# A two-layer graph network on one core: the second eviction of a transpose, a small copy, and the marks that pace a transform

## The chip, the cores and the metric

The kernel runs on one core of a Trainium2 chip. A core has four engines that matter here: TensorE (PE in the profile: matrix products and transposes), VectorE (DVE), ScalarE (ACT) and GpSimd (POOL). SyncE (SP) only issues transfers. Each engine runs its own queue of instructions in order, and waits where an operand or a buffer isn't ready. The metric is the device time of one execution in microseconds (us).

## What is computed

There are 64 graphs of 256 nodes with 256 channels, all in f32. Layer 0 multiplies by a normalised adjacency matrix and by a weight, adds the input, and applies layernorm. Layer 1 has a convolution over the nodes, a distance-weighted message sum, and a GRU cell. Cut to its core, layer 1 reads:

```python
xc = jnp.transpose(x, (0, 2, 1))
h = relu(_bn(_conv1d(xc, conv1_w, 0), ...))
h = _bn(_conv1d(h, conv2_w, 8), ...)              # 17 taps along the nodes
x_conv = jnp.transpose(relu(h + xc), (0, 2, 1))
s = x @ w_se.T + b_se                             # 3 columns
sq = jnp.sum(s * s, axis=-1)
dist = sq[:, :, None] + sq[:, None, :] - 2.0 * jnp.einsum('bnd,bmd->bnm', s, s)
A = jnp.exp(-dist) * mask
msg = relu(x @ w_msg.T + b_msg)
x_nmp = jnp.einsum('bnm,bmd->bnd', A, msg)
x_in = jnp.concatenate([x_conv, x_nmp], axis=-1)
# GRU cell with input x_in and state x, residual, layernorm
```

## The kernel before

**Tiles and stages.** A tile has 128 partitions, so a graph of 256 nodes is two chunks, and the 256 channels are two halves. The 64 graphs are worked in four quarters of 16. The 17-tap convolution of a quarter is done as a transform in 48 points: each graph's `dft` (L485) fills its columns of `V`, twelve steps of products (L544) multiply by the transformed taps, and a transform back on VectorE (`complex_end`, with outputs stored by SP at L731) gives `xc_d`. The GRU (`gru`, L842 to L921) then takes the quarter graph by graph.

**Software pipeline.** The stages of neighbouring quarters overlap. `graphs` (L970) interleaves the pieces of layer 1 of graph g with the pieces of layer 0 of graph g+2. The graphs of quarter 0 run up to about 305 us. Then quarter 0's product steps run with three pieces of the next graphs in each, to about 420 us. Then come the rest of those graphs (up to graph 27) with the transform back paced between them, to about 533 us. In the later quarters the GRU of a quarter (`late`), six graphs of the next (`begin`) and the transform back run together. The last quarter has no graphs left: only GRU and transform back. While V is in use, the next graphs' dft goes into a second tile `V2` (twelve graphs in quarter 0, six later), and `copies` (L1069) moves it to V by ScalarE copies at L1075 at the end of the transform back.

**One graph of layer 1.** `x1_transposed` (L428) transposes layer 0's result on PE (L434) into one PSUM bank and evicts it in two halves into `xn`. ScalarE evicts half 0 at L435, with a scale and a bias per partition that set one channel to a constant (the row that carries the biases). ScalarE evicts half 1 at L436 with a plain copy. `layer1` then runs conv (L451: 256 columns for h and 3 for s, in one bank for each chunk of nodes), evicts h with a ReLU (ScalarE L454) and copies the three s columns into four column groups of `scols` (VectorE L455). It squares and sums s (VectorE L459, L461, L462), computes msg (L470, evicted at L473), dft (L485, evicted at L490), transposes scols (`p_rows`, L498, evicted at L500 by ScalarE and L502 by VectorE), computes the distances (L509, L510, L511), and the message sum (`p_nmp`, L518, evicted at L522).

**Layer 0 around it.** Adjacency sums (ScalarE L362), transposes (`p_adjT` L384, evicted at L385), the scaled input (L397), products `p_hT` (L405, L410) and `p_out` (L415, L420). A `layernorm` follows, which passes from VectorE (L326 to L328) to GpSimd (power -0.5, L329), back to VectorE (L337) and to ScalarE (L339, two instructions). That x, two graphs ahead, isn't the one that conv reads at that time, but both layernorm and evictions are in the same queues.

**Banks.** The pool `ps` has four PSUM banks in rotation. Within a graph dft's first bank is the one that conv's first chunk had, so dft waits until both readers of conv, L454 and L455, are done.

**Order.** A scheduler places the instructions; the order of the code is a wish for it. Hard order comes from data and buffers, and from `tc.issue_after(op)`, which puts the instructions traced inside it behind `op` where they are on the same engine as `op`. `mark(op, gates)` notes an operation. `paced` (L952) adds, for each mark, a rate to an account (`RATES`, L1065: one rate for marks of graphs, one for marks of the GRU), and for each whole piece due it traces one piece of the transform back, or one copy L1075, behind the marked operation. Marked per graph are the two additions L420, the two ReLUs L454, msg's ReLU L473 and the product L511; in a GRU step the copy L869 (on ScalarE), and VectorE's L876, L898 and L916. Small weight preparations of the GRU (L1021, L1030) also go behind the latest mark.

Of the kernel before, what the change touches and what calls it, by code (L numbers as in the profile page):

```python
# [10 lines left out]
AF = mybir.ActivationFunctionType  # L11
ALU = mybir.AluOpType
AX = mybir.AxisListType

P = 128
# [11 lines left out]
def kernel(  # L27
# [27 lines left out]
    nc = tc.nc  # L55
    B, N, D = x.shape
    TAPS = conv2T.shape[1]
    PAD = TAPS // 2
    NSE = w_seT.shape[1]
# [22 lines left out]
    def bank(name):  # L82
        return ps.tile([P, 512], F32, tag="bank", name=name)

    def accbank(name):
        return psacc.tile([P, 512], F32, tag="acc", name=name)
# [4 lines left out]
    def mark(op, gates=0):  # L91
        marks.append((op.ins, gates))
# [47 lines left out]
    unit, others_only = ident[:, 0:1], const.tile([P, 1], F32, name="others_only")  # L140
# [287 lines left out]
    def x1_transposed(g):  # L428
        x1 = X1.pop(g)
        xn = XN[g] = work.tile([P, 2 * DCH, N], F32, name="xn")  # L430
        p = bank("p_x1T").rearrange("p (k n) -> p k n", k=DCH)
        for k in range(DCH):
            for c in range(NCH):
                nc.tensor.transpose(p[:, k, c * P : (c + 1) * P], x1[:, c, k * P : (k + 1) * P], ident)  # L434
        nc.scalar.activation(xn[:, 0], p[:, 0], AF.Identity, bias=unit, scale=others_only)  # L435
        nc.scalar.copy(xn[:, 1], p[:, 1])  # L436

    def layer1(g, place):

        if g not in XN:  # L440
            x1_transposed(g)
        xn, adjT = XN.pop(g), ADJT.pop(g)
        x1T = xn[:, :DCH]
        yield

        h = work.tile([P, NCH, D], F32, name="h", bufs=1)
        cols = scols.rearrange("p c (q r) -> p c q r", r=32)
        for c in range(NCH):
            p = bank("p_conv1")[:, : D + NSE]
            for k in range(DCH):  # L450
                nc.tensor.matmul(  # L451
                    p, x1T[:, k, c * P : (c + 1) * P], wc1[:, k, :], start=k == 0, stop=k == DCH - 1
                )
            mark(nc.scalar.activation(h[:, c, :], p[:, :D], AF.Relu))  # L454
            nc.vector.tensor_copy(cols[:, c, :, :NSE], p[:, D:].unsqueeze(1).to_broadcast([P, 4, NSE]))  # L455

        s3 = cols[:, :, 0, :NSE]
        sq3 = small.tile([P, NCH, NSE], F32, name="sq3")
        nc.vector.scalar_tensor_tensor(sq3, s3, -1.0, s3, op0=ALU.mult, op1=ALU.mult)  # L459
        nsq = small.tile([P, NCH], F32, name="nsq")  # L460
        nc.vector.tensor_reduce(nsq, sq3, AX.X, ALU.add)  # L461
        nc.vector.tensor_scalar(  # L462
            cols[:, :, 2:4, NSE], nsq.unsqueeze(2).to_broadcast([P, NCH, 2]), 0.5, None, op0=ALU.mult
        )
        yield
        msg = work.tile([P, NCH, D], F32, name="msg", bufs=1)
        p = bank("p_msg").rearrange("p (c d) -> p c d", c=NCH)
        for c in range(NCH):
            for k in range(DCH):
                nc.tensor.matmul(  # L470
                    p[:, c, :], x1T[:, k, c * P : (c + 1) * P], wmsg[:, k, :], start=k == 0, stop=k == DCH - 1
                )
        mark(nc.scalar.activation(msg, p, AF.Relu))  # L473
        yield


        mid = GT // 2
        if TILES[0] is not V:
            AWAY.append(place)
        for k in range(DCH):  # L480
            p = bank("p_dft")

            for c, t0, t1 in ((0, 0, mid + 1), (1, mid - 1, GT)):
                first = t0 + 1 - c * mid
                nc.tensor.matmul(  # L485
                    p[:, t0 * FL : t1 * FL], h[:, c, k * P : (k + 1) * P],
                    fwd[:, first : first + t1 - t0, :].rearrange("p t f -> p (t f)"),
                    start=c == 0, stop=True, skip_group_check=c == 1,
                )
            nc.scalar.copy(  # L490
                TILES[0][:, :, k, place * GT : (place + 1) * GT],
                p[:, : GT * FL].rearrange("p (t f) -> p f t", f=FL),
            )

        yield
        p = bank("p_rows")
        for c in range(NCH):
            nc.tensor.transpose(p[:, c * P : (c + 1) * P], scols[:, c, :], ident)  # L498
        dl = work.tile([64, N], F32, name="dist_l", bufs=1)
        nc.scalar.copy(dl, p[0:64, :N])  # L500
        dr = work.tile([64, N], F32, name="dist_r", bufs=1)
        nc.vector.tensor_copy(dr, p[64:P, :N])  # L502
        yield

        aT = work.tile([P, NCH, 2, P], F32, name="aT", bufs=1)
        for c in range(NCH):
            rows = slice(32 * c, 32 * c + 32)
            p = bank("p_dist")[:, :N]
            nc.tensor.matmul(p, dl[rows, c * P : (c + 1) * P], dr[rows, :], start=True, stop=True)  # L509
            nc.scalar.activation(aT[:, c].rearrange("p n q -> p (n q)"), p, AF.Exp, bias=nsq[:, c : c + 1], scale=2.0)  # L510
        mark(nc.vector.tensor_mul(aT, aT, adjT[:, :, 0:3:2, :]))  # L511
        yield
        if g in ALONE:
            x1_transposed(g + 1)
        p = bank("p_nmp").rearrange("p (k n) -> p k n", k=DCH)
        for k in range(DCH):
            for mc in range(NCH):
                nc.tensor.matmul(  # L518
                    p[:, k, :], msg[:, mc, k * P : (k + 1) * P], aT[:, mc].rearrange("p n q -> p (n q)"),
                    start=mc == 0, stop=mc == NCH - 1,  # L520
                )
        nc.scalar.copy(xn[:, DCH:], p)  # L522
        nc.scalar.dma_start(xn_d[g], xn)
        yield
# [21 lines left out]
    def half(p):  # L546
        return p.rearrange("p (j o) -> p j o", j=2)
# [294 lines left out]
    def gru(g):  # L842
# [5 lines left out]
        trz = gate.tile([P, 4, D], F32, name="trz", bufs=1)  # L848
# [11 lines left out]
        p15, p26 = accbank("p_rz"), accbank("p_rz")  # L860
# [5 lines left out]
        if following:  # L866
            sent(g + 1)
        first = gate.tile([P, 2, D], F32, name="first", tag="gn")
        mark(nc.scalar.copy(first, half(p15)), 1)  # L869
        nc.vector.tensor_add(trz[:, 0:2], first[:, 0:1].to_broadcast([P, 2, D]), half(p26))  # L870
        p7, p34 = accbank("p_rz"), accbank("p_rz")
        block(p7, 0, S[:, 2], T3)
        block(p34, 0, S[:, 3], B22)
# [10 lines left out]
        for c in range(NCH):  # L884
# [5 lines left out]
            p = accbank("p_n")  # L890
# [79 lines left out]
    def graphs(first, part, others):  # L970


        for i in part:
            load(first + i + 3)
            given = {"layer0": layer0(first + i + 2) if first + i + 2 < B else iter(()), "other": others[i]}
            for piece, _ in enumerate(layer1(first + i, i)):
                yield
                for name in PLACES[piece]:
                    if next(given[name], "end") != "end":
                        yield  # L980
            yield from given["other"]
# [64 lines left out]
    def gates(q, part):  # L1046

        for i in part:
            if i == 0:
                load_conv(q * Q)  # L1050
                load_gate(q * Q)
                yield
                load_conv(q * Q + 1)
                sent(q * Q)
                yield
                transposed(q * Q)
                yield
                input_sums(q * Q)
                yield
            yield from gru(q * Q + i)  # L1060
# [18 lines left out]
    for q in range(NQ):  # L1079
        first = (q + 1) * Q  # L1080
# [100 lines left out]
```

## Time and profile before

| what | value |
|---|---|
| median of 3 runs | 2153.79 us (2152.71 to 2159.55) |
| the profiled execution | 2154.62 us |
| its span in the trace | 2152.8 us |
| mean granted TensorE clock | 0.989 |

Busy time by stage, from the trace's windows (us):

| stage | from, to | PE | DVE | ACT | POOL |
|---|---|---|---|---|---|
| graphs of quarter 0 | 0, 305 | 266.49 | 139.02 | 169.81 | 120.40 |
| products of quarter 0 | 305, 420 | 113.73 | 85.53 | 44.37 | 12.21 |
| transform back, paced | 420, 533 | 99.70 | 80.47 | 67.80 | 25.69 |
| next graphs, first GRU | 533, 600 | 56.82 | 28.36 | 35.10 | 27.52 |
| quarter 1 | 600, 1060 | 447.27 | 313.14 | 183.99 | 137.39 |
| its end | 1060, 1170 | 106.89 | 53.20 | 57.09 | 33.88 |
| quarter 2 | 1170, 1660 | 476.33 | 322.97 | 204.73 | 145.99 |
| quarter 3 | 1660, 2153 | 476.27 | 369.67 | 137.15 | 194.19 |

The difference between a stage's length and its PE time is what PE stood idle. In the lines of the profile below, "L451" is line 451 of the kernel before, `out<-in` are tiles by their names, `x8` is the number of instructions, and a bracket at the end of a line gives the engine's idle time before it and the operation that ended it. In a table of groups the numbers are the busy time in us, the mean of one in ns, and the idle time before the group with its releasers.

### The profile page before, as it was taken

The numbers are of one execution on the slowest core, as the hardware profiler recorded it, in microseconds if no ns is written. First come the engines' busy times: TensorE is split into PE (matmuls) and PEld (weight loads), VectorE is DVE, ScalarE is ACT, GpSimd is POOL, SyncE is SP. The second block draws the span as 40 slices with busy tenths as digits, with TensorE's granted clock in tenths as the row PEclk, the third lists the DMA queues.
The fourth block names the chain that finished last, engine by engine and source line by source line (L and its number), as shares of the span: only waits on it lengthen the run. The fifth ranks groups of instructions, "written<-read, shape, count | busy, mean of one in ns | idle before, by whom it ended". The sixth has DMA issues, their size and how long they took to land. (4 is left out here: it accounts for less than half of the span.)

```text
span 2152.8 us, 29120 instructions
## 1 busy us (share of the span) xinstructions
PE 2043.5 (95%) x9693; PEld 1739.9 (81%) x9693; DVE 1392.4 (65%) x3531; ACT 900.0 (42%) x2049; POOL 697.3 (32%) x672
## 2 busy tenths in 40 slices
PE   6999999988899999999999999999999999999998
PEld 5777778876788888777888888877878888888887
DVE  5444458766457887764445878775544889976665
ACT  4566553456442223455554123445554122233332
POOL 3444411122332234223322223323232114355553
PEclk9999999999899999999999999999999999999999
DMA  4666556534437644334334664334332755443331
GB/s 126 212 196 194 164 162 222 173 128 137 108 103 215 204 127 128 125 102 109 104 103 147 207 190 117 113 118 122 104 98 71 240 164 143 112 123 98 88 95 49
DMA packets 302916, 298.23 MB, mean 139 GB/s; under 512 B 84112, under 2 KB 281572, under 8 KB 302766
## 3 DMA queue, kind: packets, MB, share of 16 engines
q1 hardware_dynamic: 242814, 200.37, 31.0%
q10 hardware_dynamic: 44480, 67.39, 9.0%
q0 software_dynamic: 15472, 28.61, 6.0%
q8 instruction: 77, 1.26, 0.2%
q14 instruction: 73, 0.60, 0.1%
HBM read 193.19 MB, written 103.06 MB: 138 GB/s over the span
## 5 line engine op out<-in xcount | busy, mean ns | idle before, releaser
L856 PE MATMUL p_rz<-wrz,sums 128*128 128x256 f32 x1536 | 350.7, 381 | 4.1 <-DVE gn L899 4.1
L893 PE MATMUL p_n<-wn,inputs 128*128 128x256 f32 x1536 | 351.7, 382 | 0.1
L856 PEld LDWEIGHTS p_rz<-wrz,sums 128*128 128x128 f32 x1536 | 291.2, 191 | 47.1 <-issue 8.2
L893 PEld LDWEIGHTS p_n<-wn,inputs 128*128 128x128 f32 x1536 | 289.0, 191 | 43.6 <-issue 6.3
L856 PE MATMUL p_rz<-wrz,inputs 128*128 128x256 f32 x1152 | 271.4, 380 | 1.9 <-ACT inputs L818 1.9
L856 PEld LDWEIGHTS p_rz<-wrz,inputs 128*128 128x128 f32 x1152 | 217.9, 190 | 31.6 <-ACT inputs L818 2.1
L329 POOL TENSOR_TENSOR ln_rs<-ln_rs,neg_half 128x2 f32<-128x2 f32 x129 | 98.6, 764 | 417.4 <-DVE ln_rs L328 363.0
L544 PE MATMUL p_k<-u,VM 128*128 128x256 f32 x736 | 174.5, 380 | 1.5 <-DVE VM L587 0.9
L905 ACT ACTIVATE nn<-gn 128x256 f32<-128x256 f32 x128 | 53.3, 417 | 278.6 <-DVE gn L902 278.4
L451 PE MATMUL p_conv<-wc,xn 128*128 128x259 f32 x512 | 134.9, 397 | 34.5 <-ACT xn L436 29.1
L375 POOL TENSOR_TENSOR dis<-deg,neg_half 128x2 f32<-128x2 f32 x64 | 47.7, 746 | 351.7 <-DVE deg L373 338.3
L835 POOL TENSOR_TENSOR sums<-inputs 128x384 f32<-128x384 f32 x64 | 65.1, 1018 | 285.8 <-ACT inputs L826 224.5
L544 PEld LDWEIGHTS p_k<-u,VM 128*128 128x128 f32 x736 | 138.8, 190 | 21.7 <-DMA u<-ud 1.6
L398 POOL TENSOR_TENSOR x_t<-x_t,b_t 128x512 f32<-128x512 f32 x64 | 86.2, 1347 | 183.1 <-ACT x L397 127.5
L451 PEld LDWEIGHTS p_conv<-wc,xn 128*128 128x128 f32 x512 | 95.1, 193 | 60.6 <-ACT xn L436 39.6
L485 PE MATMUL p_dft<-fwd,h 128*128 128x240 f32 x512 | 117.5, 373 | 18.5 <-DVE scols L455 18.5
L339 ACT ACTIVATE x_g<-x_g,ln_mr,ln_rs 128x256 f32<-128x256 f32 x128 | 70.0, 593 | 146.5 <-DVE ln_mr L337 146.5
L405 PE MATMUL p_hT<-adjT,x 128*128 128x256 f32 x512 | 125.3, 389 | 3.8 <-DVE adjT L387 1.5
L470 PE MATMUL p_msg<-wmsg,xn 128*128 128x256 f32 x512 | 124.7, 388 | 0.2 <-ACT inputs L826 0.2
L415 PE MATMUL p_out<-w,hT 128*128 128x256 f32 x512 | 123.3, 384 | 1.6 <-ACT hT L410 0.7
L511 DVE TENSOR_TENSOR aT<-aT,adjT 128x512 f32<-128x512 f32 x64 | 44.3, 692 | 121.1 <-ACT aT L510 121.1
L485 PEld LDWEIGHTS p_dft<-fwd,h 128*128 128x128 f32 x512 | 97.3, 192 | 30.9 <-DVE scols L455 22.8
(164 smaller groups left out, 3840.9 us busy)
## 6 DMA issues: line engine op xcount, KB each, us to landing
u<-ud SPq DMA_DIRECT2D x284, 256.0 KB
xn_d<-xn ACTq DMA_DIRECT2D x64, 512.0 KB
inputs<-xn_d SPq DMA_DIRECT2D x64, 512.0 KB
ud<-u_set POOLq DMA_DIRECT2D x39, 480.0 KB, 5.8
adj_t<-in_adj_dram SPq DMA_DIRECT2D x64, 256.0 KB
x_t<-in_x_dram SPq DMA_DIRECT2D x64, 256.0 KB
x_d<-x ACTq DMA_DIRECT2D x64, 256.0 KB
xc_d<-VM SPq DMA_DIRECT2D x64, 256.0 KB
```

Of the source, the lines that this page charges most:

```text
L329: nc.gpsimd.tensor_tensor(rs[:, : len(chunks)], rs[:, : len(chunks)], neg_half[:, : len(chunks)], op=ALU.pow)
L339: nc.scalar.activation(y[:, c, :], y[:, c, :], AF.Identity, bias=mr[:, c : c + 1], scale=rs[:, c : c + 1])
L398: nc.gpsimd.tensor_tensor(x_t, x_t, b0_t.unsqueeze(1).to_broadcast([P, NCH, D]), op=ALU.add)
L405: nc.tensor.matmul(p[:, k, :], x1[:, mc, k * P : (k + 1) * P], adjT[:, mc, 1 - mc : 3 - mc, :].rearrange("p n q -> p (n q)"), start=mc == ...
L415: nc.tensor.matmul(p[:, c, :], hT[:, k, c * P : (c + 1) * P], w0[:, k, :], start=k == 0, stop=k == DCH - 1)
L451: nc.tensor.matmul(p, x1T[:, k, c * P : (c + 1) * P], wc1[:, k, :], start=k == 0, stop=k == DCH - 1)
L470: nc.tensor.matmul(p[:, c, :], x1T[:, k, c * P : (c + 1) * P], wmsg[:, k, :], start=k == 0, stop=k == DCH - 1)
L485: nc.tensor.matmul(p[:, t0 * FL : t1 * FL], h[:, c, k * P : (k + 1) * P], fwd[:, first : first + t1 - t0, :].rearrange("p t f -> p (t f)") ...
L544: nc.tensor.matmul(p[:, j * D : (j + 1) * D], v[:, k, :], u[:, k, :], start=k == 0, stop=k == DCH - 1)
L835: nc.gpsimd.tensor_tensor(S[:, 0], A21, A22, op=ALU.add)
L856: nc.tensor.matmul(p[:, j * D : (j + 1) * D], a[:, k], wrz[:, b, k], start=k == 0, stop=k == HALF - 1)
L893: nc.tensor.matmul(p[:, o * D : (o + 1) * D], lhsT, w, start=j == 0, stop=j == len(part) - 1)
```

## The change

Four edits:

1. The eviction of half 0 of the transposed x1 (L435) goes from ScalarE's activation to VectorE's `tensor_scalar` with the same scale and bias. The eviction of half 1 stays on ScalarE.
2. The copy of s (L455) goes from VectorE to ScalarE, behind each of h's ReLUs.
3. The two marks on h's ReLUs (ScalarE) become two marks on the last of the small operations on s (VectorE, L462).
4. In the GRU the mark on ScalarE's copy (L869) becomes a mark on the VectorE addition behind it (L870).

The lines behind L462 move down by two in the changed kernel.

```diff
@@ x1_transposed
-        nc.scalar.activation(xn[:, 0], p[:, 0], AF.Identity, bias=unit, scale=others_only)
+        nc.vector.tensor_scalar(xn[:, 0], p[:, 0], others_only, unit, op0=ALU.mult, op1=ALU.add)
         nc.scalar.copy(xn[:, 1], p[:, 1])
@@ layer1
-            mark(nc.scalar.activation(h[:, c, :], p[:, :D], AF.Relu))
-            nc.vector.tensor_copy(cols[:, c, :, :NSE], p[:, D:].unsqueeze(1).to_broadcast([P, 4, NSE]))
+            nc.scalar.activation(h[:, c, :], p[:, :D], AF.Relu)
+            nc.scalar.copy(cols[:, c, :, :NSE], p[:, D:].unsqueeze(1).to_broadcast([P, 4, NSE]))
...
-        nc.vector.tensor_scalar(
+        last = nc.vector.tensor_scalar(
             cols[:, :, 2:4, NSE], nsq.unsqueeze(2).to_broadcast([P, NCH, 2]), 0.5, None, op0=ALU.mult
         )
+        mark(last)
+        mark(last)
@@ gru
-        mark(nc.scalar.copy(first, half(p15)), 1)
-        nc.vector.tensor_add(trz[:, 0:2], first[:, 0:1].to_broadcast([P, 2, D]), half(p26))
+        nc.scalar.copy(first, half(p15))
+        mark(nc.vector.tensor_add(trz[:, 0:2], first[:, 0:1].to_broadcast([P, 2, D]), half(p26)), 1)
```

## What was predicted, before the change was run

> **What bounds the kernel now.** I read the page first, then the waits of PE, then the groups by shape, then the timeline of one graph in each stage.
>
> ```profile
> span 2152.8 us, 29120 instructions
> PE 2043.5 (95%) x9693; PEld 1739.9 (81%) x9693; DVE 1392.4 (65%) x3531; ACT 900.0 (42%) x2049; POOL 697.3 (32%) x672
> ```
>
> PE is busy for 95% of the span and executes its queue in order. The change takes no matmul away, so it can win or lose only in PE's idle time, 2152.8 - 2043.5 = 109 us. The waits of PE (total us, times, longest) say who owns it:
>
> ```profile
> PE p_conv L451 <- ACT xn L436: 29.1, 21, 2.5
> PE p_dft L485 <- DVE scols L455: 18.5, 9, 8.0
> PE p_rows L498 <- DVE scols L462: 11.9, 10, 2.2
> PE p_conv L451 <- ACT xn L435: 4.4, 6, 0.8
> PE p_rz L856 <- DVE gn L899: 4.1, 4, 1.5
> ```
>
> The change touches all of them: 33.5 us of conv waiting for the evicted transpose, 18.5 us of dft waiting for the s copy (dft reuses conv's bank), 11.9 us of rows waiting for the small sums. The prices, with busy us and mean ns, come from the groups by shape:
>
> ```profile
> L898 DVE TENSOR_TENSOR gn<-p_n,bn_t 128x256 f32<-128x256 f32 x128 | 53.4, 417 | 32.4 <-PE p_n L893 32.1
> L435 ACT ACTIVATE xn<-p_x1T,ident,others_only 128x256 f32<-128x256 f32 x64 | 36.2, 566 | 4.7 <-PE p_x1T L434 4.1 <-ACT x_g L339 0.5
> L436 ACT COPY xn<-p_x1T 128x256 f32<-128x256 f32 x64 | 22.8, 357 | 3.7 <-ACT x L339 3.5 <-ACT xn L435 0.3
> L455 DVE COPY scols<-p_conv 128x12 f32<-128x12 f32 x128 | 20.7, 167 | 89.9 <-ACT h L454 88.1
> ```
>
> One graph of quarter 0's paced stage (timeline; start, duration):
>
> ```profile
> 499.57 0.60 PE L434 MATMUL p_x1T<-ident,x 128*128 128x128 f32 x4
> 500.21 0.56 ACT L435 ACTIVATE xn<-p_x1T,ident,others_only 128x256 f32<-128x256 f32 x1
> 500.68 0.36 ACT L436 COPY xn<-p_x1T 128x256 f32<-128x256 f32 x1
> 501.74 1.91 PE L451 MATMUL p_conv<-wc,xn 128*128 128x259 f32 x8
> 502.90 0.16 DVE L328 TENSOR_SCALAR ln_rs<-ln_mv 128x2 f32<-128x2 f32 x1
> 503.14 0.81 POOL L329 TENSOR_TENSOR ln_rs<-ln_rs,neg_half 128x2 f32<-128x2 f32 x1 [8.59 <-DVE ln_rs L328]
> 503.99 0.16 DVE L337 SCALAR_TENSOR_TENSOR ln_mr<-ln_mv,ln_rs 128x2 f32<-128x2 f32 x1 [0.60 <-POOL ln_rs L329]
> 504.18 1.09 ACT L339 ACTIVATE x<-x,ln_mr,ln_rs 128x256 f32<-128x256 f32 x2 [1.66 <-DVE ln_mr L337]
> 507.01 1.89 PE L485 MATMUL p_dft<-fwd,h 128*128 128x240 f32 x8 [1.19 <-DVE scols L455]
> ```
>
> The two evictions lie right behind the transposes, 0.7 us ahead of conv's turn. The next graph's layernorm (DVE, POOL, DVE, ACT) ends only at 505.3. That chain is what an eviction must not stand behind. In the first 300 us it already does:
>
> ```profile
> 107.47 1.09 ACT L339 ACTIVATE x<-x,ln_mr,ln_rs 128x256 f32<-128x256 f32 x2 [2.39 <-DVE ln_mr L337]
> 108.47 0.35 ACT L436 COPY xn<-p_x1T 128x256 f32<-128x256 f32 x1
> 108.87 1.14 PE L451 MATMUL p_conv<-wc,xn 128*128 128x259 f32 x4 [0.96 <-ACT xn L436]
> 542.63 3.57 PE L485 MATMUL p_dft<-fwd,h 128*128 128x240 f32 x8 [7.95 <-DVE scols L455]
> ```
>
> The last line is the largest single wait: 7.95 us, in which ACT runs the twelve copies L1075 ahead of h.
>
> [...] ACT is busy for 42% and DVE for 65%, so what blocks PE is the place of an instruction in a queue, not the load of the queue. [...] L898 measured 417. [...] L436 (no pointer) and L435 (two) differ by 209 ns[...].
>
> **The change part by part.**
>
> *L435 to DVE.* Not in the trace in this form. [...] upper 453 (DVE's tensor_scalar with a pointer over 128x128 at L186); I take 0.43, beside L898's 417. Moved: 64 x 0.566 = 36 us off ACT, 64 x 0.43 = 27 us onto DVE. Neither engine is full, so the sum is worth nothing by itself; the place counts.
>
> *s copy to ACT.* 12 elements; the slope between ACT's 256 and 512 element copies, (584 - 357)/256 = 0.89 ns, gives 357 - 244 x 0.89 = 0.14[...]. I take 0.17: 128 x 0.17 = 22 us onto ACT, 128 x 0.167 = 21 us off DVE. It stands right behind each h, so dft's wait for a DVE busy with transform pieces goes: 18.5 us less the 7.95, which the copies make and not DVE, is 10.6 us. The first s copy puts 0.17 ahead of the second h; PE is then in adjT and msg (2.5 us), which hides it. In the last stage nothing covers it, but no conv runs there.
>
> *The marks.* Pieces of the transform are put in behind marked instructions of the mark's own engine. An ACT mark put no order on DVE's pieces; now they stand behind L462, and in the GRU behind L870. So L459, L461 and L462 are no longer interleaved with pieces, and of rows' 11.9 us I count 7 as gone where the graph itself isn't later. SP's queue carries the pieces' stores L731 and u loads; both follow their pieces, six u buffers stand between a load and its product, and p_k waits only 2.1 us for DMA in the whole span, so nothing there. ACT's copies L1075 lose their marks and float.
>
> *The order.* Set against before, the built program's queues tell more than the diff. In quarter 0's paced stage L435 stands on DVE behind the other graph's L328 in graphs 21 and 24, behind its L337, and so behind POOL, and one or two pieces, in 20, 23, 25, 26 and 27. On ACT, L436 stands behind both L339, where it led them. Behind L436 on ACT are h and L385, behind L435 on DVE are pieces and L420; PE has conv, adjT and msg queued behind both.
>
> By stage:
> 1. To 305 us: L436 stays behind L339; L435 comes behind L328 (105.34 + 0.16), so ends near 105.95 with conv due at 106.00. 0 (-2 to +2).
> 2. Graphs 16 to 19: L435 can be behind V pieces that wait for PE. +0.5 (0 to +3).
> 3. Graph 20: conv from 415.75 to L339's end 421.2 at most, less a little since conv's first half needs only L435: about 420.85. Then conv, adjT and msg (4.4) put dft at 425.5 for 419.67, +5.8; hT's wait for L397 of 1.38 and rows' 0.2 go. +4 (+3 to +5).
> 4. Graphs 21 to 27: from x1T to dft takes 6.1, 7.5, 7.2, 7.7, 7.2, 7.4, 7.3 now, 50.4 in all. In the example L339 would end at 505.3, L436 at 505.65 and the second halves of conv at 505.8; conv's end, then msg's 1.9, give dft at 509.3, 9.75 behind x1T instead of 7.4. So for each: 9.35, 9.0, 10.85, 9.0, 9.95, 9.75, 9.25, together 67.15, +16.8. From dft to the next x1T the 49.7 us become 46.6, since the waits of rows go: -3.1. Sum +13.6 (+8 if the layernorm comes earlier because DVE has no pieces there, +18 if POOL's L398 holds it).
> 5. End of quarter 0: three of the twelve copies now stand ahead of L436, nine ahead of h. The 7.95 splits into a wait of conv and one of dft. +0.5 (0 to +1.5).
> 6. Quarters 1 and 2: dft's two waits of 1.80 and rows' go; L436 moves ahead of the other layernorm in graphs 42, 44, 58, 60 and 62 (its waits were 1.33, 0.95, 1.68, 0.94). Per quarter: -1.8 -1.1 -0.4 -1.33 -0.95, against +0.5 +0.85 +0.8 and 4 x 0.2: -2.6; two of them -5.5 with 0.3 for smaller gaps (-9 to +4).
> 7. Last quarter: no graph, same GRU; pieces behind L870 shift by under 1 us. 0 (-1 to +1).
>
> Sum: 0.5 + 4 + 13.6 + 0.5 - 5.5 = +13. The profiled execution took 2154.62 (span 2152.8 and 1.8 around it), 0.8 above the median of the runs, 2153.79; 2153.8 + 13 = 2167. The low ends add to -1, the high ends to +34.5: 2153 to 2188.
>
> **The rivals.**
> - *Shorter after all.* L435 on DVE and L436 on ACT run side by side, 0.5 us earlier than in turn; dft's 10.6 and 7 of rows' 11.9 go: 2154 - 17.6 = 2136. For it: the waits really vanish. Against: it needs both evictions ahead of the layernorm chain, which the queues of quarter 0 contradict. Not slower than before; it decides if L436's lead over L339 costs under 0.3 us a graph.
> - *No change.* The moved stalls weigh as much as those removed: item 4 at +6 with item 6 at -9, or the layernorm, with fewer pieces in its way, ends 1 us earlier: 2154 within 5.
> - *Worse.* L435 is late in the 32 graphs of quarters 1 and 2 too. A DVE operation beside a POOL addition can stretch: L716 took 1.41 us at 507.93 beside L398, 0.42 alone. With 0.6 us for each of 32 graphs, +19: 2186.
>
> **How the numbers follow.** Forecast 0.60, shorter 0.11, no change 0.16, worse 0.13. A measurement of this kernel tells about 0.3%, 6.5 us, from no change: 2147.3 to 2160.3. Of the forecast's 0.60 a twelfth falls in that band. Faster 0.11, same 0.19, slower 0.70. The range 2150 to 2186 leaves out most of "shorter" and half of "worse".
>
> **What would show it.** In the changed kernel's waits of PE: L485 for L455 nearly gone; conv for L436 up from 29 to 50 us or more, mostly between 415 and 540 us, with L339 the releaser ahead of L436 on ACT; L455 on ACT near 170 ns and L435 on DVE near 430. The stage 400 to 550 us should be longer by some 17 us, 600 to 1660 shorter by some 5. The forecast is wrong if conv starts within 1 us of x1T's end in graphs 21 to 27, or if quarters 1 and 2 change by more than 10 us either way.

## The result, and the profile after

The changed kernel is slower: 2181.88 us median of four runs (2175.36 to 2183.55), against 2156.67 us (2152.71 to 2164.02) for the kernel before. The ratio is 1.0107, with a 95% interval of 1.0071 to 1.0144, so the loss is about 23 us (15 to 31). The profiled execution of the changed kernel is the fastest of its four, 2175.36 us; 20.8 us of the difference in span can be placed in it.

The page of the changed kernel, its first lines:

```profile
span 2173.6 us, 29350 instructions
PE 2050.7 (94%) x9693; PEld 1737.8 (80%) x9693; DVE 1414.1 (65%) x3467; ACT 882.0 (41%) x2113; POOL 693.9 (32%) x672
```

Span minus PE's busy time was 109.3 us and is now 122.9. So 13.6 of the 20.8 us are added idle time; the other 7.2 us are longer matmuls. The engines' loads moved the way intended (ScalarE down by 18 us, VectorE up by 22), and that bought nothing. Its waits of PE (total us, times, longest):

```profile
PE p_conv L451 <- DVE xn L435: 30.4, 19, 4.7
PE p_conv L451 <- ACT xn L436: 26.2, 21, 3.0
PE p_hT L405 <- DVE adjT L387: 14.6, 16, 1.9
...
PE p_dist L511 <- DVE dist_r L504: 5.8, 5, 3.1
...
PE p_dft L487 <- ACT scols L455: 2.4, 1, 2.4
PE p_rows L500 <- DVE scols L462: 2.0, 1, 2.0
```

dft's and rows' waits on these copies and sums, 30.4 us before, are down to 4.4: the s copy on ScalarE does that. But conv waits 56.6 us for the two evictions instead of 33.5, and a wait that was 1.5 us before, hT for the diagonal of adjT (L387), is 14.6. The groups of the moved operations:

```profile
L435 DVE TENSOR_SCALAR xn<-p_x1T,others_only,ident 128x256 f32<-128x256 f32 x64 | 33.9, 529 | 1.0 <-PE p_x1T L434 1.0
L436 ACT COPY xn<-p_x1T 128x256 f32<-128x256 f32 x64 | 22.9, 357 | 13.3 <-DVE xn L435 10.9 <-ACT x L339 2.0
L455 ACT COPY scols<-p_conv 128x12 f32<-128x12 f32 x128 | 22.2, 173 | 0.6 <-issue 0.6
```

The middle line has the surprise: ahead of L436, the half that stayed on ScalarE, ScalarE sat idle 10.9 us for L435 on VectorE. The two halves are on two engines, and still L436 starts after L435's end in 64 of 64 graphs of this trace, the nearest time 0.03 us after it. One graph of the paced stage, from the timeline (start, duration; the bracket is idle time and its releaser):

```profile
509.89 0.60 PE L434 MATMUL p_x1T<-ident,x 128*128 128x128 f32 x4
...
513.28 0.16 DVE L328 TENSOR_SCALAR ln_rs<-ln_mv 128x2 f32<-128x2 f32 x1
...
514.37 0.16 DVE L337 SCALAR_TENSOR_TENSOR ln_mr<-ln_mv,ln_rs 128x2 f32<-128x2 f32 x1 [0.60 <-POOL ln_rs L329]
514.44 0.42 DVE L635 SCALAR_TENSOR_TENSOR turn<-VM 128x256 f32<-128x256 f32 x1
514.56 1.09 ACT L339 ACTIVATE x<-x,ln_mr,ln_rs 128x256 f32<-128x256 f32 x2 [1.72 <-DVE ln_mr L337]
514.78 0.54 DVE L435 TENSOR_SCALAR xn<-p_x1T,others_only,ident 128x256 f32<-128x256 f32 x1
...
515.37 1.14 PE L451 MATMUL p_conv<-wc,xn 128*128 128x259 f32 x4 [3.15 <-DVE xn L435]
515.56 0.35 ACT L436 COPY xn<-p_x1T 128x256 f32<-128x256 f32 x1
```

x1T is done at 510.5, and nothing but the queue keeps L435 until 514.78: the other graph's layernorm and a piece of the transform stand ahead of it. Conv idles for 3.15 us, and the second eviction comes behind the first and behind L339.

To place the loss I compare one milestone of each graph, the start of the eviction of p_nmp on ScalarE (64 in each trace), and the last tanh of the GRU. Each column is the change of (this kernel minus before) across a stretch of graphs, in us, all worked out from the timelines of the profiled executions:

| kernel | to graph 12 | 12-15 | 15-19 | 19-20 | 20-27 | 27-31 | 31-47 | 47-63 | to the end | sum |
|---|---|---|---|---|---|---|---|---|---|---|
| changed | -1.2 | -3.8 | -0.3 | +4.2 | +15.4 | +0.9 | +2.2 | +1.4 | +1.9 | +20.8 |
| e1: edit 1 | -1.5 | -3.8 | 0 | +5.6 | +12.7 | 0 | +0.6 | -2.5 | -0.4 | +10.8 |
| e2: edit 2 | +4.0 | 0 | -0.2 | -0.2 | -3.0 | -0.3 | +0.3 | +1.7 | -1.7 | +0.7 |
| e3: edits 3, 4 | +3.4 | 0 | 0 | -0.2 | +3.8 | +0.4 | +4.0 | +6.4 | 0 | +17.8 |
| e6: edit 3 | +4.2 | 0 | 0 | -0.2 | +3.8 | +0.9 | +5.7 | +4.9 | -1.4 | +17.9 |
| e4: 2, 3, 4 | +0.5 | 0 | -0.1 | -1.1 | +10.5 | +0.1 | +0.5 | -3.6 | +0.5 | +7.4 |
| e5: 1, 2 | -1.5 | -3.8 | -0.2 | +5.9 | +12.6 | +2.0 | +2.1 | -0.1 | -1.4 | +15.8 |
| e12: 1, 2, 3 | +4.0 | -3.8 | -0.2 | +5.4 | +16.6 | +1.2 | +1.8 | +6.3 | +0.1 | +31.4 |
| e8: all, early | +3.6 | -3.8 | +0.3 | -0.3 | +6.2 | +2.6 | +2.9 | +5.6 | +0.6 | +17.8 |
| e10: 1, 2, early | -1.2 | -3.8 | +0.3 | +0.6 | +0.4 | +0.6 | +3.7 | +0.5 | -0.8 | +0.3 |
| e11: e10, copies | +3.7 | -3.8 | +0.2 | +0.6 | +0.4 | -3.5 | +2.9 | +2.6 | -1.8 | +1.4 |
| e9: 2, copies | -1.6 | 0 | -0.2 | -0.2 | -1.4 | -4.9 | +0.6 | -1.8 | +1.7 | -7.7 |
| e13: all, two banks | -7.0 | -7.0 | +0.1 | +5.6 | +15.6 | +1.8 | -6.9 | +1.8 | +1.6 | +5.7 |

The first column is in part no property of a kernel. Some executions go through the first 70 us at a lower TensorE clock. Windows 30 to 48 and 48 to 70 us of the kernel before (length, busy us of PE, PEld, DVE, ACT, POOL, then the clock, DMA share and GB/s):

```profile
30.00:48.00 18.00, 17.27 (x83) 14.20 (x82) 8.45 (x22) 10.04 (x27) 4.63 (x5) 0.93 0.32 92
48.00:70.00 22.00, 19.13 (x95) 15.85 (x94) 10.40 (x28) 11.72 (x27) 10.01 (x9) 1.00 0.55 178
```

and of the kernel with edit 2 alone:

```profile
30.00:48.00 18.00, 17.27 (x75) 14.02 (x74) 6.13 (x17) 10.40 (x29) 2.82 (x4) 0.82 0.34 93
48.00:70.00 22.00, 19.14 (x85) 15.56 (x84) 8.14 (x19) 10.92 (x27) 8.62 (x9) 0.92 0.51 164
```

PE is equally busy but gets fewer matmuls done. The edits don't explain it: e2 and e9 are the same program up to 500 us and stand at +4.0 and -1.6, e10 and e11 at -1.2 and +3.7. So about 5 us of a single execution are chance here, one reason why these sums and the ratios of many runs differ. From graph 12 on, the columns are steadier: all kernels with edit 1 on one bank show -3.8 in "12-15", all without it 0.

The columns "19-20" and "20-27", which hold most of the loss, are not waits alone. The same stretch in windows, before and then changed:

```profile
415.95:531.75 115.80, 102.50 (x502) 81.99 (x501) 83.77 (x272) 68.48 (x169) 26.55 (x26) 1.00 0.39 129
410.70:546.07 135.37, 107.78 (x496) 85.02 (x496) 90.59 (x262) 66.39 (x176) 24.34 (x24) 0.96 0.33 109
```

Of the 19.6 us, 14.3 are added idle time of PE, and 5.3 are longer matmuls: slightly fewer of them take longer, at a mean clock of 0.96 where it was 1.00.

### The profile page after: what moved, and what is told of

It is laid out like the page before. It is cut to its first block, busy times and chain, and to the rows that moved or that the text cites. A ratio compares the mean times of both kernels' runs of the same rounds, so it can differ in the third digit from the quotient of the medians.

```text
span 2173.6 us, 29350 instructions
## 1 busy us (share of the span) xinstructions
PE 2050.7 (94%) x9693; PEld 1737.8 (80%) x9693; DVE 1414.1 (65%) x3467; ACT 882.0 (41%) x2113; POOL 693.9 (32%) x672
## 4 chain that ended last, share of the span: by engine, by line
PE 51%; DVE 7%; issue 5%; POOL 5%; ACT 3%; DMA 2%; ACTq 0%; SPq 0%; POOLq 0%; DVEq 0%
PE p_rz L858 20%; PE p_n L895 11%; PE p_k L546 7%; PE p_hT L405 2%; PE p_out L415 2%; PE p_conv L451 2%; PE p_msg L472 2%; PE p_dft L487 2%; PE p_nmp L520 1%; DMA u<-ud 1%; POOL ln_rs L329 1%; PE p_dist L511 1%; POOL sums L838 1%; POOL sums L842 1%; POOL sums L837 1%
## 5 line engine op out<-in xcount | busy, mean ns | idle before, releaser
L451 PE MATMUL p_conv<-wc,xn 128*128 128x259 f32 x512 | 138.1, 401 | 57.7 <-DVE xn L435 30.4
L405 PE MATMUL p_hT<-adjT,x 128*128 128x256 f32 x512 | 129.8, 396 | 15.6 <-DVE adjT L387 14.6
L398 POOL TENSOR_TENSOR x_t<-x_t,b_t 128x512 f32<-128x512 f32 x64 | 84.6, 1322 | 155.8 <-ACT x L397 101.3
L520 PE MATMUL p_nmp<-aT,msg 128*128 128x256 f32 x512 | 122.1, 382 | 0.2 <-DVE aT L513 0.2
L339 ACT ACTIVATE x_g<-x_g,ln_mr,ln_rs 128x256 f32<-128x256 f32 x128 | 70.0, 593 | 128.6 <-DVE ln_mr L337 128.6
L405 PEld LDWEIGHTS p_hT<-adjT,x 128*128 128x128 f32 x512 | 95.7, 198 | 32.9 <-DVE adjT L387 6.7
```

Source lines behind the costliest of these rows:

```text
L339: nc.scalar.activation(y[:, c, :], y[:, c, :], AF.Identity, bias=mr[:, c : c + 1], scale=rs[:, c : c + 1])
L398: nc.gpsimd.tensor_tensor(x_t, x_t, b0_t.unsqueeze(1).to_broadcast([P, NCH, D]), op=ALU.add)
L405: nc.tensor.matmul(p[:, k, :], x1[:, mc, k * P : (k + 1) * P], adjT[:, mc, 1 - mc : 3 - mc, :].rearrange("p n q -> p (n q)"), start=mc == ...
L451: nc.tensor.matmul(p, x1T[:, k, c * P : (c + 1) * P], wc1[:, k, :], start=k == 0, stop=k == DCH - 1)
L520: nc.tensor.matmul(p[:, k, :], msg[:, mc, k * P : (k + 1) * P], aT[:, mc].rearrange("p n q -> p (n q)"), start=mc == 0, stop=mc == NCH - 1,)
```

## The experiments

Ratios are to the kernel before, with 95% intervals.

**e1: edit 1 alone**

```diff
-        nc.scalar.activation(xn[:, 0], p[:, 0], AF.Identity, bias=unit, scale=others_only)
+        nc.vector.tensor_scalar(xn[:, 0], p[:, 0], others_only, unit, op0=ALU.mult, op1=ALU.add)
```

> The kernel before with edit 1 alone (half 0 of the transpose evicted by VectorE; s copy and marks as before). Queue theory (the loss comes from where the eviction stands: behind the other graph's layernorm on VectorE, with L436 behind L339 on ScalarE): 15 to 30 us above before, conv's waits for L435 and L436 together 50 us or more, dft's and rows' waits still there. Marks theory (the loss comes from transform pieces put behind L462 and so ahead of L387 and L502): within 6 us of before. Price theory (VectorE's eviction is simply dearer and VectorE fuller): 15 to 30 us above, too.

Measured: 1.0064 (1.0041 to 1.0088), about 14 us, just below the range expected. Conv's waits for L435 and L436 are 30.7 and 20.5 us, as expected, and graphs 19 to 27 lose 18.3 us, nearly the whole loss of the changed kernel there (19.6). The marks theory falls as the only cause. The price theory expected the same time, so this run alone doesn't part it from the queue theory; e8 and e10 do.

**e2: edit 2 alone**

```diff
-            nc.vector.tensor_copy(cols[:, c, :, :NSE], p[:, D:].unsqueeze(1).to_broadcast([P, 4, NSE]))
+            nc.scalar.copy(cols[:, c, :, :NSE], p[:, D:].unsqueeze(1).to_broadcast([P, 4, NSE]))
```

> The kernel before with edit 2 alone (s copied by ScalarE behind h's ReLUs). All theories: dft's waits for the s copy lose the 10 us that VectorE's queue made, the wait of 8 us behind the copies L1075 stays; rows may wait longer for L462 instead. Total 3 to 12 us below before; conv's waits unchanged near 33 us.

Measured: 0.9990 (0.9979 to 1.0002), a gain of 2 us that can't be told from none and is less than the 3 to 12 expected. dft's waits fall from 18.5 to 9.5 us, 7.8 of it the wait behind the copies L1075. The paced stage gains 3.0 us where dft's waits lost 9: hT's wait for L387 rises from 1.5 to 2.8 us and rows still waits 8.8.

**e4: edits 2, 3 and 4, without edit 1**

```diff
-        nc.vector.tensor_scalar(xn[:, 0], p[:, 0], others_only, unit, op0=ALU.mult, op1=ALU.add)
+        nc.scalar.activation(xn[:, 0], p[:, 0], AF.Identity, bias=unit, scale=others_only)
```

(against the changed kernel)

> The changed kernel without edit 1: both halves evicted by ScalarE as before, s copy on ScalarE, marks moved. Queue theory: 0 to 12 us below before, conv's waits back near 33 us or less, hT's waits for L387 present. Marks theory: 14 to 25 us above before, as the changed kernel. Price theory: as the queue theory.

Measured: 1.0026 (1.0014 to 1.0038), 6 us slower: between the two theories. With the eviction back on ScalarE most of the loss goes, and a part stays that the eviction can't make. Its waits of PE:

```profile
PE p_hT L405 <- DVE adjT L387: 27.6, 20, 2.8
PE p_conv L451 <- ACT xn L436: 24.4, 19, 2.3
```

Conv's waits are below before, and hT's wait for L387 is the largest of all. Where it comes from, in a graph of the paced stage (timeline of the same kernel):

```profile
512.08 0.17 DVE L462 TENSOR_SCALAR scols<-nsq 128x4 f32<-128x4 f32 x1
...
513.07 1.76 POOL L398 TENSOR_TENSOR x_t<-x_t,b_t 128x512 f32<-128x512 f32 x1 [2.34 <-issue]
...
513.62 1.49 DVE L718 SCALAR_TENSOR_TENSOR VM<-VM 128x256 f32<-128x256 f32 x1
515.03 0.68 DVE L714 SCALAR_TENSOR_TENSOR VM<-turn,VM 128x512 f32<-128x512 f32 x1
...
516.57 0.34 DVE L387 SCALAR_TENSOR_TENSOR adjT<-ident,adeg,adjT 128x128 f32<-128x128 f32 x1
...
516.96 1.17 PE L405 MATMUL p_hT<-adjT,x 128*128 128x256 f32 x3 [2.79 <-DVE adjT L387]
```

The pieces that the moved marks release behind L462 stand ahead of the second L387, 4.5 us after L462. One of them, L718, takes 1.49 us beside POOL's L398; its median in this trace is 0.42.

**e8: the changed kernel with the transposes issued one piece earlier**

```diff
-        yield
         if g in ALONE:
             x1_transposed(g + 1)
+        yield
```

> The changed kernel with the transposes of graphs 17 to 28 issued one piece earlier, ahead of layer 0's p_out, so that L435 stands ahead of L420 and of the layernorm in VectorE's queue in quarter 0's paced stage. Everything else as in the changed kernel. Queue theory: conv's waits for L435 between graphs 20 and 28 fall from 20 us to under 5, and the total is 8 to 16 us below the changed kernel's. Price theory: the same eviction at the same price, so no change beyond 3 us. Marks theory: no change beyond 3 us.

Measured: 1.0063 (1.0039 to 1.0087), so 1.0063/1.0107 = 0.9956 of the changed kernel, 9.5 us less, as the queue theory had it, though the two intervals overlap, so that the size is uncertain. Conv's waits for L435 between graphs 20 and 28 are gone (from 20.2 us to none). The price theory falls: the eviction is the same, on the same engine. But graphs 20 to 27 still lose 6.2 us. Two waits are new there: h on ScalarE now waits for the layernorm, and hT waits for L387. The first in the timeline:

```profile
509.90 1.09 ACT L339 ACTIVATE x<-x,ln_mr,ln_rs 128x256 f32<-128x256 f32 x2 [2.81 <-DVE ln_mr L337]
510.89 0.36 ACT L454 ACTIVATE h<-p_conv 128x256 f32<-128x256 f32 x1
```

Which of the two costs is told by e10 below, which has the first without the second.

**e3: edits 3 and 4 alone**

```diff
-            mark(nc.scalar.activation(h[:, c, :], p[:, :D], AF.Relu))
+            nc.scalar.activation(h[:, c, :], p[:, :D], AF.Relu)
...
+        mark(last)
+        mark(last)
...
-        mark(nc.scalar.copy(first, half(p15)), 1)
-        nc.vector.tensor_add(trz[:, 0:2], first[:, 0:1].to_broadcast([P, 2, D]), half(p26))
+        nc.scalar.copy(first, half(p15))
+        mark(nc.vector.tensor_add(trz[:, 0:2], first[:, 0:1].to_broadcast([P, 2, D]), half(p26)), 1)
```

> The kernel before with edits 3 and 4 alone (marks moved to L462 and to the GRU's VectorE addition; evictions and s copy as before). If the moved marks put transform pieces between L462 and L387 on VectorE whoever copies s: hT's waits for L387 of 15 to 28 us, mostly between graphs 20 and 28, and 3 to 14 us above before. If the marks matter only once ScalarE copies s: within 3 us of before and hT's waits under 5 us.

Measured: 1.0090 (1.0062 to 1.0118), 19 us, more than expected, and in another place. hT's waits are 11.1 us, and the paced stage loses only 3.8 us; quarters 1 and 2 lose 10.4. There p_out waits for hT's eviction (3.3 us in each quarter, which before didn't show) and conv for L436 (3.1 us), and the mean clock from 1500 to 1530 us is between 0.77 and 0.88. So the moved marks alone cost about as much as edit 1 alone, but the two don't add: all four edits cost 23 us.

**e6: edit 3 alone** (e3 without the edit to the GRU's mark)

```diff
-            mark(nc.scalar.activation(h[:, c, :], p[:, :D], AF.Relu))
+            nc.scalar.activation(h[:, c, :], p[:, :D], AF.Relu)
...
+        mark(last)
+        mark(last)
```

> The kernel before with edit 3 alone (layer 1's marks moved to L462, the GRU's mark left). Edits 3 and 4 together cost 19 us. If layer 1's marks make the loss: 10 to 20 us above before, hT's waits for L387 near 9 us between graphs 20 and 28, and the loss of quarters 1 and 2 (10 us from graph 31 to 63) there as well. If the GRU's mark makes the loss of quarters 1 and 2: 3 to 10 us above before, and graphs 31 to 63 within 2 us of before.

Measured: 1.0063 (1.0035 to 1.0091), 14 us; hT's waits are 8.9 us between graphs 20 and 28, as expected, and graphs 31 to 63 lose 10.6 us. Layer 1's marks make the loss. In quarters 1 and 2 it isn't hT's wait for L387, though, which is only 1.6 us there; p_out waits 5.8 us there for hT's eviction, which it didn't before. Why the marks bring that about wasn't followed.

**e12: the changed kernel without edit 4**

```diff
-        nc.scalar.copy(first, half(p15))
-        mark(nc.vector.tensor_add(trz[:, 0:2], first[:, 0:1].to_broadcast([P, 2, D]), half(p26)), 1)
+        mark(nc.scalar.copy(first, half(p15)), 1)
+        nc.vector.tensor_add(trz[:, 0:2], first[:, 0:1].to_broadcast([P, 2, D]), half(p26))
```

> The changed kernel without edit 4 (the GRU's mark stays on ScalarE's copy). If the GRU's mark costs something in quarters 1 to 3: graphs 31 to 63 and the end 3 us or more shorter than in the changed kernel. If not: the same within 2 us in each quarter, and the total that of the changed kernel.

Measured: 1.0140 (1.0114 to 1.0167), not below the changed kernel but above it; the intervals overlap. Neither expected outcome came: "47-63" is 4.9 us longer than in the changed kernel. Beside edit 3 alone, edit 4 seemed to add 6 us (e3 against e6), and here taking it away adds 7. It has no clear price of its own.

**e5: edits 1 and 2, marks as before** (against the changed kernel; the GRU's mark goes back as in e12)

```diff
-            nc.scalar.activation(h[:, c, :], p[:, :D], AF.Relu)
+            mark(nc.scalar.activation(h[:, c, :], p[:, :D], AF.Relu))
...
-        mark(last)
-        mark(last)
```

> The changed kernel with the marks where they were before (edits 1 and 2 alone). Queue theory (the eviction's place costs, the marks add little on top, since a late conv covers them): conv's waits for L435 near 20 us between graphs 20 and 28 as in edit 1 alone, hT's waits for L387 under 5 us, total 8 to 16 us above before. Were the marks an equal part of the changed kernel's loss: 11 us or more below the changed kernel, within 12 us of before.

Measured: 1.0107 (1.0078 to 1.0137), the same as the changed kernel: on top of a late eviction the moved marks cost nothing that can be told (the intervals are 0.3 to 0.4% wide to each side). With the marks back, hT waits for L387 1.6 us in all, none of it in the paced stage. In the changed kernel it waits 4.4 us there, against 13.4 in e4, which has the same marks without the late eviction. A likely reading, not shown, is that VectorE works off the pieces while conv waits for L435 anyway.

**e10: edits 1 and 2 and the earlier transposes** (against e5)

```diff
-        yield
         if g in ALONE:
             x1_transposed(g + 1)
+        yield
```

> Edits 1 and 2 with marks as before, and the transposes of graphs 17 to 28 issued one piece earlier, ahead of p_out. Queue theory: both causes, the eviction behind the layernorm and the pieces ahead of L387, are gone, so conv's waits between graphs 20 and 28 are under 3 us, hT's waits under 5 us, and the total is within 5 us of before. If VectorE's load or the eviction's price were what costs: 8 us or more above before.

Measured: 1.0003 (0.9990 to 1.0016). Against e5 the same operations run on the same engines; only the transposes are traced ahead of p_out for twelve graphs, and with them their evictions ahead of L420 and the layernorm. That is worth 1.0% of the time, 22 us. In graphs 19 to 27 the loss goes from 18.5 to 1.0 us. The waits of PE in the stretch "20-27" of the table, in e8 and then in e10, which differ in edits 3 and 4:

```profile
PE p_dft L487 <- ACT scols L455: 9.7, 7, 1.7
PE p_hT L405 <- DVE adjT L387: 8.4, 9, 2.0
...
PE p_dft L485 <- ACT scols L455: 9.6, 7, 1.7
PE p_rows L498 <- DVE scols L462: 2.6, 4, 0.9
PE p_hT L405 <- DVE adjT L387: 0.5, 1, 0.5
```

dft's wait for h behind the layernorm is the same in both, and e10 loses 0.4 us in this stretch where e8 loses 6.2. So what e8 still loses there comes with hT's wait for L387, that is with the moved marks. In the total, e8 is 1.0060 of e10, 13 us, and their intervals lie apart: once the eviction is in time, the moved marks do cost.

**e9: edit 2, and every second copy L1075 on VectorE** (against e2)

```diff
-        for i in waiting:
-            nc.scalar.copy(V[:, :, :, i * GT : (i + 1) * GT], V2[:, :, :, i * GT : (i + 1) * GT])
+        for n, i in enumerate(waiting):
+            copy = nc.vector.tensor_copy if n % 2 else nc.scalar.copy
+            copy(V[:, :, :, i * GT : (i + 1) * GT], V2[:, :, :, i * GT : (i + 1) * GT])
```

> Edit 2 alone, and every second of the copies from V2 to V (L1075) done by VectorE instead of ScalarE. The wait of dft behind twelve copies in a row (8 us) falls to about 4 us, so the total is 3 to 7 us below edit 2 alone and 4 to 9 us below before. No gain if the copies on VectorE run into something else, such as L459 for rows.

Measured: 0.9966 (0.9956 to 0.9977), 7 us below before, as expected: the one version here that beats both kernels clearly. The end of quarter 0 in its timeline:

```profile
529.28 2.90 DVE L1076 COPY VM<-V 128x768 f32<-128x768 f32 x6 [0.44 <-issue]
529.90 0.82 ACT L1076 COPY VM<-V 128x768 f32<-128x768 f32 x1
530.62 3.76 ACT L1076 COPY VM<-V 128x768 f32<-128x768 f32 x5
...
534.76 1.57 PE L485 MATMUL p_dft<-fwd,h 128*128 128x240 f32 x3 [3.40 <-ACT scols L455]
```

dft waits 3.40 us for the 7.8 of e2. VectorE does its six in 2.90 us, 0.48 each, where ScalarE needs 4.5 us, so an uneven share might be better still; that wasn't tried.

**e11: e10 with the shared copies of e9** (against e10)

```diff
-            nc.scalar.copy(V[:, :, :, i * GT : (i + 1) * GT], V2[:, :, :, i * GT : (i + 1) * GT])
+            copy = nc.vector.tensor_copy if n % 2 else nc.scalar.copy
+            copy(V[:, :, :, i * GT : (i + 1) * GT], V2[:, :, :, i * GT : (i + 1) * GT])
```

> Edits 1 and 2, marks as before, transposes of graphs 17 to 28 one piece earlier, and every second copy L1075 on VectorE. Against the same without the shared copies (0.03% from before): 4 to 6 us less, from dft's wait behind the copies, so 3 to 7 us below before. If the copies' wait is merely replaced by the layernorm in front of h: no gain beyond 2 us.

Measured: 0.9995 (0.9986 to 1.0004): a miss. The 4 us come where they should ("27-31" is -3.5 for +0.6), but they can't be told in the total: against e10 "47-63" is 2.1 us worse, with conv's waits for L435 up from 10.0 to 19.7 us in all, as the schedule of quarters 1 and 2 changed as well. Why it changed is open.

**e13: the changed kernel with the halves of the transpose in two PSUM banks**

```diff
-        p = bank("p_x1T").rearrange("p (k n) -> p k n", k=DCH)
+        p = [bank(f"p_x1T{k}") for k in range(DCH)]
...
-                nc.tensor.transpose(p[:, k, c * P : (c + 1) * P], x1[:, c, k * P : (k + 1) * P], ident)
-        nc.vector.tensor_scalar(xn[:, 0], p[:, 0], others_only, unit, op0=ALU.mult, op1=ALU.add)
-        nc.scalar.copy(xn[:, 1], p[:, 1])
+                nc.tensor.transpose(p[k][:, c * P : (c + 1) * P], x1[:, c, k * P : (k + 1) * P], ident)
+        nc.vector.tensor_scalar(xn[:, 0], p[0][:, :N], others_only, unit, op0=ALU.mult, op1=ALU.add)
+        nc.scalar.copy(xn[:, 1], p[1][:, :N])
```

> The changed kernel with the two halves of the transpose in two PSUM banks instead of one. In the changed kernel L436 on ScalarE never starts before L435 on VectorE has ended (64 of 64 graphs, the nearest 0.03 us later), and it carries a wait for VectorE. If the shared bank is what ties them: L436 starts before L435 ends in most graphs, conv's waits for L436 in the first 300 us fall from 12.7 us to under 3 and in all from 26 us to under 12, L435's between graphs 20 and 28 stay near 20 us since its place on VectorE is the same; total 8 to 20 us below the changed kernel. If the tie comes from the shared tile xn or from ScalarE's queue: no change beyond 4 us. One more bank of the four per graph could add waits for a bank elsewhere, up to 5 us.

Measured: 0.9990 (0.9976 to 1.0004), which is 0.9884 of the changed kernel, 25 us less, more than expected: with the four edits unchanged, the time is back at that of the kernel before. L436 now starts before L435 has ended in 63 of 64 graphs, and conv's waits for L436 fall from 26.2 us to a single one of 0.7, which the kernel before has at the same place (0.7 at 33 us). The tile xn and ScalarE's queue, the other readings, are as before in this run, so they don't make the tie. Two graphs of its timeline, one of the first 300 us and one of the paced stage:

```profile
104.75 0.38 ACT L436 COPY xn<-p_x1T 128x256 f32<-128x256 f32 x1
105.20 0.54 DVE L435 TENSOR_SCALAR xn<-p_x1T,others_only,ident 128x256 f32<-128x256 f32 x1
...
106.23 1.92 PE L451 MATMUL p_conv<-wc,xn 128*128 128x259 f32 x8
...
107.27 1.09 ACT L339 ACTIVATE x<-x,ln_mr,ln_rs 128x256 f32<-128x256 f32 x2 [2.15 <-DVE ln_mr L337]
...
502.55 0.37 ACT L436 COPY xn<-p_x1T 128x256 f32<-128x256 f32 x1
...
506.74 0.54 DVE L435 TENSOR_SCALAR xn<-p_x1T,others_only,ident 128x256 f32<-128x256 f32 x1
...
507.43 2.77 PE L451 MATMUL p_conv<-wc,xn 128*128 128x259 f32 x8 [3.19 <-DVE deg L373]
```

In the first graph L436 leads L339, and conv runs its eight in one go: the 0.96 us that it lost at most of these graphs before are gone. Up to 305 us conv waits 3.9 us in all, for 20.7 in the kernel before and 18.2 in the changed one. The last three lines show the other cause untouched: in the paced stage L435 still stands behind the layernorm, and conv waits for it (the bracket names another VectorE operation; L435 is the one that ends at 507.28). So graphs 19 to 27 still lose 21.2 us against before, and the gain is elsewhere: 14.0 us to graph 15 and 6.9 in quarter 1. The two banks don't take the change's loss away, then; they take away a wait that the kernel before has as well, where ScalarE evicts both halves in turn, and that offsets the loss. This kernel's profiled execution, 2160.34 us, is slower than its median of 2153.70, at a mean clock of 0.982 for 0.989 before. Two things come along with the second bank and weren't tried apart: a tile of this pool is one bank, so the run doesn't tell whether the program keeps the order by bank or by tile, and each graph takes one bank more from the rotation of four.

## Why the prediction held, and where it did not

The direction and the range held: 2167 (2150 to 2186) was forecast and 2182 measured. In the profiled execution the sum is +20.8 for +13. That the sum came so close is in part luck: items 1, 6 and 7 miss by -5.0, +9.1 and +1.9 us, and partly cancel. The shares given to the four outcomes also add to 0.21 for the same and 0.68 for slower, where 0.19 and 0.70 were put. By the steps:

- **The waits of dft and the s copy: right.** L455 on ScalarE takes 173 ns for the 170 taken (an estimate; the trace of before alone gave 140), and its wait is gone but for one of 2.4 us. What e2 adds is that this was worth little by itself.
- **The price of L435: wrong.** 0.43 was taken and 0.453 the upper end; it takes 529 ns on average (505 to 545). The 0.43 was an estimate set beside the 417 ns of L898, which has no pointer operand. The upper end was no bound: the 453 at L186 are a mean of six over half as many elements, of which the median is 286 and one took 1299. A nearer relative was in the trace, with one pointer operand and from PSUM:

```profile
L420 DVE SCALAR_TENSOR_TENSOR x<-p_out,dis,x_t 128x256 f32<-128x256 f32 x128 | 56.6, 478 | 14.2 <-PE p_out L415 13.3
```

  The 0.1 us matter little where L435 is 3 us late.
- **Items 3 and 4, graphs 20 to 27: right in the queues, and near in the sum.** +4.2 for +4 and +15.4 for +13.6. L435 stands behind L337 in just the graphs named, 20, 23, 25, 26 and 27, and L436 behind both L339 in all eight. e8 and e10 show that this place costs, since conv's waits go when the eviction comes ahead of the layernorm and, with the marks back, the loss goes too. From x1T to dft the seven graphs take 65.5 us, for 67.15 forecast and 50.4 before. From dft to the next x1T they were to take 3.1 us less, because rows' waits go; they take 1.3 more, since hT's waits for L387 come in their place. The forecast counted waits alone, and part of what came is longer matmuls at a lower clock. The wait carries L435's name, too, not L436's as was said.
- **Item 1, to 305 us: too high.** 0 was forecast; -5.0 came. Of this -1.2 lie before graph 12 and can be chance, and -3.8 came at graphs 13 to 15, in every kernel with edit 1 on one bank. There conv waited six times for an eviction, 7.70 us in all, and now waits five times, 5.82 us. The other half of the gain is a stretch at half the clock that the kernel before has there and the changed one hasn't:

```profile
257.00:261.20 4.20, 2.02 (x10) 1.59 (x11) 0.56 (x5) 1.34 (x3) 2.48 (x5) 1.00 0.98 312
261.20:264.60 3.40, 3.40 (x10) 2.67 (x9) 1.36 (x7) 2.04 (x5) 0.85 (x1) 0.50 0.87 267
264.60:268.00 3.40, 3.40 (x18) 3.08 (x18) 0.26 (x1) 1.81 (x4) 0.42 (x1) 1.00 0.06 22
```

  In the middle window PE has 10 matmuls at a clock of 0.50, in the next, as long, 18 at 1.00.
- **Items 2, 5 and 7: small, as forecast.** -0.3, +0.9 and +1.9 came for +0.5, +0.5 and 0; items 2 and 7 lie just outside their ranges. p_k's waits for its loads, where the forecast saw nothing to come, went from 2.1 to 4.2 us.
- **Item 6, quarters 1 and 2: the step that failed.** -5.5 was forecast and +3.6 measured. The gains of dft and rows did come: dft's wait there is gone, and rows' is down from 3.8 to 0.6 us a quarter. Conv's waits, of which 2.3 us a quarter were to go where L436 moves ahead of the other layernorm, stayed: 13.6 us in the two quarters before, 13.4 now, since L435's (4.8) come in the place of what L436's lost. And two waits have no named term in the item. The pieces behind L462 delay L387, and hT waits 4.3 us in each quarter for it (not at all in e5, where the marks stay); I counted the small sums as freed and didn't ask what stands behind the pieces. dist waits 2.0 and 3.7 us more, most of it for L504, VectorE's half of the eviction of rows, which starts only after ScalarE's half has ended (64 of 64 graphs, at the nearest 0.03 us later). The windows of the two quarters (graphs 31 to 47 and 47 to 63), before and then changed:

```profile
643.10:1166.90 523.80, 508.33 (x2427) 434.73 (x2427) 340.75 (x848) 219.62 (x504) 157.68 (x153) 0.99 0.45 133
1166.90:1669.10 502.20, 488.37 (x2341) 417.28 (x2341) 329.71 (x821) 209.36 (x476) 147.12 (x142) 1.00 0.44 132
658.40:1184.40 526.00, 509.79 (x2428) 434.58 (x2427) 343.69 (x832) 215.37 (x521) 157.39 (x153) 0.99 0.45 132
1184.40:1688.00 503.60, 487.66 (x2341) 415.96 (x2340) 332.35 (x805) 205.09 (x492) 146.52 (x142) 1.00 0.44 131
```

  PE is as busy as before (997.5 us for 996.7) at the same clock, so it is the waits: idle time goes from 29.3 to 32.2 us. hT's waits alone don't explain it: e4 has 6.3 us of them in each quarter, no edit 1, and its two quarters are 3.1 us shorter than before. Nor do the marks, since e5, with them as before, has +2.0 us there. How the waits replace one another in these quarters stays open.

**The rival "shorter after all"** assumed that the halves run side by side. I judged it by the queues, which was right for quarter 0, and didn't see why L436 was behind L339 at all: it came behind L435. With both halves in one bank L436 starts after L435's end in 64 of 64 graphs; with two banks it starts before L435's end in 63 of 64 (e13). Why is not shown. The same order is in the kernel once more: in the kernel before, L502 on VectorE starts after L500 on ScalarE has ended in 64 of 64 graphs, though the two read different partitions of their bank; no run moves these two into different banks. With the tie of L435 and L436 gone, the time is 2154, no change, and not this rival's 2136: the eviction is still late in quarter 0.

**The rival "worse"** (L435 late in quarters 1 and 2 by 0.6 us a graph, +19) didn't come: conv's waits for L435 there add to 4.8 us.

So the loss has two causes that cover one another. One is the eviction's place behind the layernorm: 18 us in graphs 19 to 27 (e1, e5), and 1.0 once the place is changed (e10). The other is the moved marks: 14 us alone (e6), 13 with the eviction in time (e8 against e10), nothing that can be told beside the late eviction (e5). In the paced stage they cost through the pieces ahead of L387; in quarters 1 and 2 of e6 through other waits, and that part is open. The tie of the two halves is a third cost, of 25 us (e13), but for the most part not one that the change brought in. Taking it away brings the time back to before by gaining elsewhere; taking away the place alone saves about 9.5 us (e8), and with the marks put back as well, all of it (e10). How they would add in other mixtures isn't settled; e11 shows that the scheduler's order changes with small edits.

## What to carry to other kernels

Where two halves of a tile are to be evicted by two engines, look whether they share a PSUM bank: here they ran in turn in 64 of 64 graphs, the second inherited the place of the first in another engine's queue, and two banks were worth 25 us, for one bank more in use. Work out an eviction's cost from what stands ahead of it in the new queue, and whose chain of engines that waits for; its own 0.5 us is the small part. When filler work is hung behind a new operation, look at what was next behind that operation, because that is what the filler delays.

## What the runs showed of the hardware that I had not expected

- VectorE's `tensor_scalar` with two pointer operands from PSUM, 128x256 in f32, takes 505 to 545 ns in the changed kernel (L435), where in the kernel before a two-tensor operation from PSUM of that size without a pointer (L898) takes 417 on average and one with a single pointer (L420) 478.
- VectorE copies 128x768 in f32 in 0.48 us each in a run of six (e9, 2.90 us), ScalarE in 0.75 (3.76 us for five).
- In e4 a VectorE operation with a median of 0.42 us (L718) took 1.49 beside POOL's L398, and L398 itself 1.76, where its median in the kernel before is 1.27.
- The clock record of TensorE is 0.50 in nine stretches of the kernel before: five of 3.4 us (261.2 to 264.6 us is one), two of 6.8, one of 10.2, and the last 7 us of the span, where PE has no matmul left. In the changed kernel there are eleven: nine of 3.4 us, one of 6.8, and again the last 7 us. What sets them off isn't shown. In the changed kernel conv waits 2.92 us for L436 in quarter 1 and again in quarter 2, to 997.8 and to 1512.8 us: the clock is 0.50 from 998.9 to 1002.3 us, and 1.00 from 1500 to 1530 us.
- The stretch from 30 to 70 us has a mean clock of 0.93 and 1.00 in its two windows in the kernel before, of 0.82 and 0.92 in e2. e2 and e9, the same program up to 500 us, lie 5.6 us apart at graph 12.
